# Layer 0's softmax weights made once: exponentials from the masked scores that VectorE keeps, turned by TensorE, in place of a second pass of scores

## The chip, the cores and the metric

The kernel runs on one core of a Trainium2 chip. A core has a matrix engine (TensorE, PE in the profile, with its weight loads as PEld), a vector engine (VectorE, DVE), an activation engine (ScalarE, ACT), a general engine (GpSimd, POOL) and a queue that issues transfers (SyncE, SP). Matrix products are written into PSUM, which has eight banks of 128 x 512 numbers; everything else works on SBUF. All data are 32-bit floats.

The metric is the device time of one execution in microseconds (us), the median of several runs.

## The reference, cut to what matters

Sixteen samples of 100 tokens (E = 512) pass through four layers, with a context of 361 rows for each sample. Layer 0, the only one that is changed, is a cross attention with 32 query heads in 8 groups that share keys and values, heads of 16:

```python
q = hidden_state @ Wq + bq                      # (16, 100, 512) -> 32 heads of 16
k = encoder_hidden_state @ Wk + bk              # (16, 361, 128) -> 8 heads of 16
v = encoder_hidden_state @ Wv + bv
scores = einsum('bkgld,bksd->bkgls', q, k) * scale + mask
attn = softmax(scores, axis=-1)                 # over the 361 context rows
out = einsum('bkgls,bksd->bkgld', attn, v) @ Wo + bo
x = layer_norm(out + hidden_state) * gamma + beta
```

Layers 1 and 3 are recurrent layers with a feed-forward part, layer 2 is a second cross attention with its own feed-forward. They read x as the layer ahead left it.

## The kernel before, in words

`layer0` (L238) loops over the 16 samples `b`. The queries of four samples (a group) are projected together; keys and values are projected for each sample. The 32 heads are ordered by a parity `par` (2), a chunk `q` (4) and a row group `r` (4): four heads `r` lie in four bands of 32 partitions of one tile, so that their four products run at once on four bands of PE. Four such products are called a burst here.

Before, the scores are made twice. The first pass (`maxima`, L376, eight calls for each sample, one for each `par` and `q`) makes a burst of scores 100 tokens x 361 rows; DVE adds the mask, negates, and keeps only the minimum of each row in the tile `nm`, while the masked scores go to a tile `junk` that nobody reads. `turn_maxima` (L397) turns these numbers by PE. The second pass (`weights`, L406, six calls: two parities, three blocks `j` of 121 rows) makes the scores again the other way round, with the context rows on partitions, subtracts the maximum by a second product (`msel`, `nx`) in the same bank, DVE adds the turned mask (`turn_mask`, L361), and one exponential of 121 x 1600 on ACT makes the weights `pt` of four `r` and four `q`. `attend` (L446) multiplies them with the values. The sums of the weights are made by POOL, which adds the three blocks into `pa`, and by PE (`sums`, L462, with the selector `osel`); DVE inverts them and `divide` (L484) spreads them over the channels by a product with `rsel`. `output` (L501) projects, adds the residual and normalizes.

The two passes are one sample apart: while sample `b` has its second pass, sample `b + 1` has its first. The list `ORDER` (L576) sets that order: S0 to S7 are first-pass calls, T0 to T5 second-pass calls. Ahead of the loop, the eight first-pass calls of sample 0 run alone.

All layer-0 work is recorded in program order on its engine (`mm`, `turn` and the wrappers `vector`, `scalar`, `gpsimd`, which is why nearly all rows in the profile carry the lines L77, L82 and L85). What is neither first nor second pass (projections, attends, sums, divide, output) is put into a `Filler` (L91): a list of pieces with an estimated time and the first slot in which each may stand. After each pass call the filler emits as many pieces as an equal share of the estimated total allows, and the deferred readers of their results in later slots.

PSUM in layer 0: a ring of six banks for scores (L242), one for the attended values `acc`, one for everything else. A burst takes the next four banks of the ring and writes them in the order r = 3, 2, 1, 0 (`BURST`); DVE reads them in the order 0, 1, 2, 3.

Transfers are issued by SP in program order: at the start of sample `b` the context, mask and x of sample `b + 2`.

Of the kernel before, what the change touches and what calls it, by code (L numbers as in the profile page):

```python
# [35 lines left out]
def xattn_sequence(ctx: ExitStack, tc: tile.TileContext, d: dict, out: bass.AP):  # L36
# [201 lines left out]
    def layer0(next_weights):  # L238
        with ExitStack() as es:
            one = es.enter_context(tc.tile_pool(name="l0_one", bufs=1))  # L240
            two = es.enter_context(tc.tile_pool(name="l0_two", bufs=2))
            score = psum_ring(es, "l0_sc", 6)  # L242
# [13 lines left out]
            i32 = ident.rearrange("p (r s) -> p s r", s=32)  # L256

            msel = one.tile([128, 2, KW], F32, name="l0_msel")


            osel = one.tile([KW, 8, 32], F32, name="l0_osel")

            rsel = one.tile([128, 4, 128], F32, name="l0_rsel")
            vzs = [one.tile([KW, 3, 2, 128], F32, name=f"vz{i}") for i in range(2)]
            nms = [one.tile([L, 4, 128], F32, name=f"nm{i}") for i in range(2)]

            live, qzs, xTs, last = {}, {}, {}, {}
# [53 lines left out]
            def keys(fill, b, slot=0):  # L321
                def ps():
                    live[b]["kz"] = two.tile([128, 2, S2], F32, tag="kz", bufs=3, name=f"kz_{b}")
                    t = bank(f"k_{b}")
                    return t, t[:, :S2]

                def then(t):
                    for par in range(2):
                        scalar.activation(
                            live[b]["kz"][:, par, :], t[:, :S2], AF.Identity,  # L330
                            bias=kb[:, par : par + 1], scale=par01[:, par : par + 1],
                        )

                chain(
                    fill, 0.63, slot, ps, lambda c: wk[:, c, :], lambda c: live[b]["ct"][:, c, :], then,
                    delay=0,
                )
# [23 lines left out]
            def turn_mask(fill, b, slot=0):  # L361
                mt = []

                def step():
                    mt.append(bank(f"mT_{b}"))
                    for j, (k0, _) in enumerate(KEYS):
                        turn(mt[0][:KW, j * L : (j + 1) * L], live[b]["mask"][:, k0 : k0 + KW], ident[:L, :L])

                def then():
                    t = live[b]  # L370
                    t["maskT"] = two.tile([KW, 3, L], F32, tag="maskT", bufs=3, name=f"maskT_{b}")
                    scalar.copy(t["maskT"].rearrange("p j t -> p (j t)"), mt[0][:KW, : 3 * L])

                fill.add(0.5, slot, step, then, 0, object())

            def maxima(b, x):  # L376

                par, q = x // 4, x % 4
                mask, kz = live[b]["mask"], live[b]["kz"]
                nm, qz = nms[b % 2], qzs[b // G]  # L380
                sl = slice(b % G * L, (b % G + 1) * L)
                ss = [score() for r in range(4)]
                for r in BURST:
                    rs = slice(32 * r, 32 * r + 32)
                    mm(
                        out=ss[r][:L, :S2], lhsT=qz[rs, q, sl], rhs=kz[rs, par, :],
                        start=True, stop=True,
                    )
                for r in range(4):
                    junk = two.tile([L, S2], F32, tag="junk", bufs=1, name=f"junk_{b}_{par}_{q}_{r}")  # L390
                    col = 32 * r + par
                    vector.tensor_tensor_reduce(
                        out=junk, in0=ss[r][:L, :S2], in1=mask, scale=-1.0, scalar=FLT_MAX,
                        op0=ALU.add, op1=ALU.min, accum_out=nm[:, q, col : col + 1],
                    )

            def turn_maxima(b):  # L397

                ps = bank(f"nmT_{b}")
                for q in BURST:  # L400
                    turn(ps[:, q * L : (q + 1) * L], nms[b % 2][:, q, :], ident[:L, :L])
                live[b]["nx"] = two.tile([128, T], F32, tag="nx", bufs=1, name=f"nx0_{b}")
                scalar.copy(live[b]["nx"], ps[:, :T])
                live[b]["pt"], live[b]["pa"] = {}, {}

            def weights(fill, b, k):  # L406


                par, j = k // 3, k % 3
                t = live[b]  # L410
                k0 = KEYS[j][0]
                sl = slice(b % G * L, (b % G + 1) * L)
                pt = t["pt"][k] = two.tile([KW, 4, T], F32, tag="pt", bufs=7, name=f"pt0_{b}_{k}")
                st = [score() for r in range(4)]
                for r in BURST:
                    rs = slice(32 * r, 32 * r + 32)
                    mm(
                        out=st[r][:KW, :T], lhsT=t["kz"][rs, par, k0 : k0 + KW],
                        rhs=qzs[b // G][rs, :, sl], start=True, stop=False,
                    )  # L420
                for r in range(4):
                    rs = slice(32 * r, 32 * r + 32)
                    mm(
                        out=st[r][:KW, :T], lhsT=msel[rs, par, :], rhs=t["nx"][rs, :],
                        start=False, stop=True,
                    )
                for r in range(4):
                    vector.tensor_tensor(
                        pt[:, r, :].rearrange("p (q t) -> p q t", t=L),
                        st[r][:KW, :T].rearrange("p (q t) -> p q t", t=L),  # L430
                        t["maskT"][:, j, None, :].to_broadcast([KW, 4, L]), ALU.add,
                    )

                def exp():
                    scalar.activation(pt, pt, AF.Exp)
                    if j == 1:
                        pa = t["pa"][par] = two.tile([KW, 4, T], F32, tag="pa", name=f"pa_{b}_{par}")
                        gpsimd.tensor_tensor(pa, t["pt"][k - 1], pt, ALU.add)
                    elif j == 2:
                        n = KEYS[2][1]  # L440
                        pa = t["pa"][par]
                        gpsimd.tensor_tensor(pa[:n], pa[:n], pt[:n], ALU.add)

                fill.later.append((fill.slot + 1, exp))

            def attend(fill, b, k, slot):  # L446
                par, j = k // 3, k % 3
                n = KEYS[j][1]

                def step():  # L450
                    if k == 0:
                        live[b]["acc"] = ps_acc.tile([128, 512], F32, tag="acc", name=f"acc_{b}")
                    for r in range(4):
                        rs = slice(32 * r, 32 * r + 32)
                        mm(
                            out=live[b]["acc"][rs, :T], lhsT=vzs[b % 2][:n, j, par, rs],
                            rhs=live[b]["pt"][k][:n, r, :], start=(k == 0), stop=(k == 5),
                        )

                fill.add(0.8, slot, step)  # L460

            def sums(fill, b, par, slot):  # L462
                def step(q):
                    for r in range(4):
                        rs = slice(32 * r, 32 * r + 32)
                        mm(
                            out=live[b]["acc"][rs, T : T + L], lhsT=osel[:, 4 * par + q, :],
                            rhs=live[b]["pa"][par][:, r, q * L : (q + 1) * L],
                            start=(par == 0 and q == 0), stop=(par == 1 and q == 3),
                        )  # L470

                def then():
                    t = live[b]
                    t["rinv"] = two.tile([128, L], F32, tag="rinv", name=f"rinv_{b}")
                    vector.reciprocal(t["rinv"], t["acc"][:, T : T + L])
# [3 lines left out]
                for q in range(4):  # L479
                    fill.add(  # L480
                        0.25, slot, lambda q=q: step(q), then if par == 1 and q == 3 else None, 0
                    )

            def divide(fill, b, slot):  # L484
                rb = []

                def step():
                    rb.append(bank(f"rb_{b}"))
                    for q in range(4):
                        mm(  # L490
                            out=rb[0][:, q * L : (q + 1) * L], lhsT=rsel[:, q, :], rhs=live[b]["rinv"],
                            start=True, stop=True,
# [6 lines left out]
                fill.add(1.0, slot, step, then, 1, object())  # L499

            def output(fill, b, slot):  # L501
# [6 lines left out]
                def then(t):  # L508
                    v = two.tile([L, E], F32, tag="v", bufs=1, name=f"res0_{b}")
                    vector.tensor_tensor(v, t[:L, :], xb[b], ALU.add)  # L510
                    st["v"], (st["mv"], st["rstd"]) = v, ln_stats(two, [v], 1e-6, f"0_{b}", vector, gpsimd)
                    fill.later.append((fill.slot + 5, scaled))
# [29 lines left out]
            m2 = one.tile([128, 2], F32, name="l0_m2")  # L542
            vector.tensor_reduce(m2, i32[:, 0:2, :], AX.X, ALU.add)
            vector.tensor_copy(msel, m2[:, :, None].to_broadcast([128, 2, KW]))
            for t in nms + vzs + [osel]:
                gpsimd.memset(t, 0.0)
            for i in range(8):
                gpsimd.memset(osel[:, i, i : i + 1], 1.0)
                vector.tensor_copy(
                    rsel[:, i % 4, :].rearrange("p (r h c) -> p h r c", h=2, c=16)[:, i // 4],  # L550
                    i32[:, i, :, None].to_broadcast([128, 4, 16]),
                )
            gpsimd.memset(osel[:, 0, 8:32], 1.0)
# [6 lines left out]
            turn_mask(fill, 0)  # L560
# [1226 lines left out]
```

## Time and profile before

| What | us |
|---|---|
| Median of three runs | 3452.1 (3450.18 to 3452.9) |
| Profiled execution | 3447.39 |
| Its span in the profile | 3445.6 |
| First scores of layer 0 | 29.1 |
| First pass over sample 1 begins (loop starts) | 66.0 |
| Turned maxima of sample 0, of sample 15 | 66.8, 690.8 |
| Last row of layer 0 ends, layer 1 begins | 739.1 |

Busy times over the whole span: PE 3121.5 us (91%), DVE 1753.5 (51%), ACT 977.3 (28%), POOL 1373.2 (40%).

In the rows of the timeline, the first number is the start in us from the begin of the span, the second the time from the first start to the last end, then engine, line, operation, output<-inputs, the shapes and how many instructions were merged; in brackets the idle time of the engine ahead of it and what ended it. A product of 32-bit floats is two matmul instructions, a transposition is one. In the windows, each engine's busy time in a stretch is followed by its number of instructions; PEclk is the clock granted to PE, as a share of full speed. Matmul ends are modelled and overlap, so the cost of a group on PE is best read from its start to the next group's start.

### The profile page before, as it was taken

How to read it: one execution, taken by the hardware profiler on the slowest of the kernel's cores; microseconds unless marked ns; L12 is line 12 of the kernel's file. 1: busy time of each engine (PE TensorE's matmuls, PEld its weight loads, DVE VectorE, ACT ScalarE, POOL GpSimd, SP SyncE). 2: the span in 40 equal slices, each digit the busy share in tenths (PEclk: the TensorE clock that was granted, in tenths of full speed). 3: DMA queues.
4: the chain of work that ended last, by engine and by line, in shares of the span. 5: the costliest groups of instructions: out<-in, count | busy, mean ns of one | idle time of the engine just before them, and what ended most of it. 6: DMA issues, size and time to landing. Idle time of an engine off the chain costs nothing. (4 is left out here: it accounts for less than half of the span.)

```text
span 3445.6 us, 47937 instructions
## 1 busy us (share of the span) xinstructions
PE 3121.5 (91%) x18371; PEld 1422.0 (41%) x18371; DVE 1753.5 (51%) x3570; ACT 977.3 (28%) x1715; POOL 1373.2 (40%) x1036
## 2 busy tenths in 40 slices
PE   6989898868999989988999999879998899998997
PEld 3434443334333333334455555445553433333333
DVE  4777777732877766523333333320001287766661
ACT  1333233222233333321323222211111233423332
POOL 0444444443775765521212111220002377676551
PEclk8999999979999989999999999989998999998998
DMA  5010100013335353222000000010011343535321
GB/s 173 22 31 22 31 22 34 1 32 115 113 108 150 109 173 108 77 72 64 28 19 20 19 20 31 26 64 10 10 58 34 111 129 102 150 116 174 91 70 50
DMA packets 171374, 240.18 MB, mean 70 GB/s; under 512 B 27678, under 2 KB 139358, under 8 KB 171146
## 3 DMA queue, kind: packets, MB, share of 16 engines
q1 hardware_dynamic: 148106, 204.35, 19.9%
q10 hardware_dynamic: 23040, 32.78, 2.7%
q8 instruction: 144, 2.36, 0.3%
q14 instruction: 84, 0.69, 0.1%
HBM read 174.25 MB, written 36.04 MB: 61 GB/s over the span
## 5 line engine op out<-in xcount | busy, mean ns | idle before, releaser
L77 POOL TENSOR_TENSOR a<-a,rr 128x800 f32<-128x800 f32 x256 | 480.9, 1880 | 331.0 <-DVE a L77 212.0
L77 DVE TENSOR_TENSOR_SCAN a<-wr,vb 128x400 f32<-128x400 f32 x512 | 475.9, 971 | 20.7 <-PE acc L82 9.1
L77 DVE TENSOR_TENSOR vb<-vb,kr 128x792 f32<-128x792 f32 x256 | 250.1, 977 | 184.7 <-ACT vb L77 184.5
L77 DVE CUSTOM_DVE_ANT_0 junk<-l_sc,mask 100x361 f32<-100x361 f32 x512 | 272.9, 533 | 87.1 <-PE l_sc L82 70.5
L82 PE MATMUL vb<-vc,sel 32*128 32x396 f32 x1024 | 252.7, 565 | 3.3 <-DVE a L77 3.3
L77 DVE TENSOR_TENSOR pt<-l_sc,maskT 121x400 f32<-121x400 f32 x384 | 193.4, 566 | 89.6 <-PE l_sc L82 88.8
L77 ACT ACTIVATE pt<-pt 121x1600 f32<-121x1600 f32 x96 | 147.6, 1538 | 282.4 <-DVE pt L77 280.8
L1490 DVE CUSTOM_DVE_ANT_0 junk<-l2a_sc,mask 100x361 f32<-100x361 f32 x256 | 136.9, 535 | 173.0 <-PE l2a_sc L82 155.8
L1526 POOL TENSOR_TENSOR pa<-pt,pt 121x1600 f32<-121x1600 f32 x16 | 57.1, 3569 | 362.3 <-ACT pt L1521 362.3
L77 POOL TENSOR_TENSOR xj<-tm,ext 128x400 f32<-128x400 f32 x160 | 150.6, 961 | 110.9 <-DVE tm L77 110.1
L77 DVE SCALAR_TENSOR_TENSOR tm<-mm,vec,sx 128x400 f32<-128x400 f32 x160 | 95.7, 628 | 185.5 <-PE mm L82 149.4
L82 PE MATMUL k<-ct,l_k_w 128*128 128x361 f32 x512 | 173.3, 482 | 14.4 <-DMA ct<-in_ctxT 14.4
L1707 DVE TENSOR_TENSOR x<-pb,x 100x512 f32<-100x512 f32 x16 | 12.2, 760 | 335.4 <-DMA pb<-po 330.3
L77 POOL TENSOR_TENSOR pa<-pt,pt 121x1600 f32<-121x1600 f32 x32 | 114.7, 3583 | 165.0 <-ACT pt L77 165.0
L63 PE MATMUL h<-yTb,l_fc 128*128 128x400 f32 x512 | 174.5, 503 | 6.3 <-ACT yTb L229 6.3
L82 PE MATMUL v<-l_v_w,ct 128*121 128x512 f32 x384 | 175.5, 601 | 0.0
L63 PE MATMUL p<-l_proj,h 128*128 128x512 f32 x384 | 165.5, 592 | 0.0
L77 ACT COPY vb<-s0r 128x8 f32<-128x8 f32 x256 | 42.9, 168 | 407.8 <-PE vb L82 320.4
L82 PE MATMUL l_sc<-kz,qz 32*100 32x361 f32 x1024 | 116.7, 526 | 42.9 <-DVE pt L77 22.0
L82 PEld LDWEIGHTS vb<-vc,sel 32*128 32x128 f32 x1024 | 81.9, 191 | 154.0 <-issue 113.5
L63 PEld LDWEIGHTS h<-yTb,l_fc 128*128 128x128 f32 x512 | 97.7, 192 | 81.1 <-ACT yTb L229 8.3
L77 POOL TENSOR_TENSOR pa<-pa,pt 119x1600 f32<-119x1600 f32 x32 | 114.4, 3576 | 41.1 <-ACT pt L77 40.9
(258 smaller groups left out, 5174.2 us busy)
## 6 DMA issues: line engine op xcount, KB each, us to landing
kr<-dk SPq DMA_DIRECT2D x256, 100.0 KB
wr<-dw SPq DMA_DIRECT2D x256, 100.0 KB
rr<-dr SPq DMA_DIRECT2D x256, 100.0 KB
ct<-in_ctxT SPq DMA_DIRECT2D x32, 722.0 KB
dk<-k ACTq DMA_DIRECT2D x32, 200.0 KB
kc<-dk SPq DMA_DIRECT2D x32, 200.0 KB
dw<-wd ACTq DMA_DIRECT2D x32, 200.0 KB
dv<-v ACTq DMA_DIRECT2D x32, 200.0 KB
```

The lines of the kernel that those rows point to most:

```text
L63: nc.tensor.matmul(out=ps, lhsT=lhs(c), rhs=rhs(c), start=(c == 0), stop=(c == n - 1))
L77: return lambda *args, **kw: tc.keep_in_program_order(op(*args, **kw))
L82: pin(nc.tensor.matmul(**kw))
L1490: nc.vector.tensor_tensor_reduce(out=junk, in0=ss[r][:L, :S2], in1=t["mask"], scale=-1.0, scalar=FLT_MAX, op0=ALU.add, op1=ALU.min, accum_ ...
L1526: nc.gpsimd.tensor_tensor(t["pa"], t["pt"][0], pt, ALU.add)
L1707: nc.vector.tensor_tensor(x, pb[:, i, :], x, ALU.add)
```

## The change: what it does

The second pass of scores goes, and with it `turn_mask`, `turn_maxima`, `sums`, the selectors `msel`, `osel` and `rsel` and POOL's additions. DVE's pass writes the negated masked scores into a tile `pr` (three buffers) instead of `junk`; its minima go to `nm`, 32 columns for a sample. ACT then makes the weights in place, one exponential of 100 x 361 for each head, with scale -1 and the minimum as bias, and its accumulator gives the sum of each row into `sums`. PE turns the weights (`turn_weights`): for each of the eight calls and each of the three blocks `j`, four transpositions of 100 x 121 into one bank of a new ring of two (`l0_pT`). ACT copies blocks 0 and 2 into `pt`, DVE copies block 1. `attend` is as before. `invert` inverts the 32 sums of a token on DVE, POOL spreads them over 16 channels each (`rx`), and `divide` turns that by PE.

The score ring has four banks instead of six; the two others are the new ring. The loop goes over the samples once, one burst for each of eight steps x, with the turning of a step one step behind; a seventeenth pass through the loop finishes the last sample. There is no run of sample 0 ahead of the loop: values of samples 0 and 1, keys of sample 1 and the product of the value bias stand in the first sample. Keys have two buffers instead of three and are made one sample ahead instead of two.

```diff
-            score = psum_ring(es, "l0_sc", 6)
+            score = psum_ring(es, "l0_sc", 4)
+            turned = psum_ring(es, "l0_pT", 2)
...
+            def scores(b, x):
                 par, q = x // 4, x % 4
...
                 ss = [score() for r in range(4)]
                 for r in BURST:
                     rs = slice(32 * r, 32 * r + 32)
                     mm(
+                        out=ss[r][:L, :S2], lhsT=qzs[b // G][rs, q, sl], rhs=t["kz"][rs, par, :],
                         start=True, stop=True,
                     )
+                pr = two.tile([L, 4, S2], F32, tag="pr", bufs=3, name=f"pr_{b}_{x}")
+
+                def maximum(r):
+
+                    col = 8 * q + 2 * r + par
+                    vector.tensor_tensor_reduce(
+                        out=pr[:, r, :], in0=ss[r][:L, :S2], in1=t["mask"], scale=-1.0, scalar=FLT_MAX,
+                        op0=ALU.add, op1=ALU.min, accum_out=t["nm"][:, col : col + 1],
+                    )
+
+                def exp(r):
+                    col = 8 * q + 2 * r + par
+                    scalar.activation(
+                        pr[:, r, :], pr[:, r, :], AF.Exp, bias=t["nm"][:, col : col + 1], scale=-1.0,
+                        accum_out=t["sums"][:, col : col + 1],
+                    )
+
+                return pr, maximum, exp
+
+            def turn_weights(b, x, pr, j):
+
+                par, q = x // 4, x % 4
+                t = live[b]
+                if q == 0 and j == 0:
+                    t["pt", par] = two.tile([KW, 3, 4, T], F32, tag="pt", name=f"pt0_{b}_{par}")
+                ps = turned()
+                k0 = KEYS[j][0]
                 for r in range(4):
+                    turn(ps[:KW, r * L : (r + 1) * L], pr[:, r, k0 : k0 + KW], ident[:L, :L])
+                return lambda copy: copy(
+                    t["pt", par][:, j, :, q * L : (q + 1) * L],
+                    ps[:KW, :T].rearrange("p (r t) -> p r t", t=L),
+                )
...
+            def invert(b):
+
+                t = live[b]
+                rinv = two.tile([L, 32], F32, tag="rinv", name=f"rinv_{b}")
+                vector.reciprocal(rinv, t["sums"])
+                t["rx"] = two.tile([L, E], F32, tag="rx", bufs=1, name=f"rx_{b}")
+                gpsimd.tensor_copy(
+                    t["rx"].rearrange("p (h c) -> p h c", c=16), rinv[:, :, None].to_broadcast([L, 32, 16])
+                )
...
+                for x in range(8):
+                    now = (b, x, *scores(b, x)) if b < B else None
+                    if now:
+                        pr, maximum, exp = now[2:]
+                        maximum(0)
+                        maximum(1)
+                    due = fill.run(3 * x, due + share)
+                    if last:
+                        turn_weights(*last[:3], 0)(scalar.copy)
+                    if now:
+                        exp(0)
+                        exp(1)
+                        maximum(2)
+                    due = fill.run(3 * x + 1, due + share)
+                    if last:
+                        turn_weights(*last[:3], 1)(vector.tensor_copy)
+                    if now:
+                        maximum(3)
+                    if last:
+                        turn_weights(*last[:3], 2)(scalar.copy)
+                    if now:
+                        exp(2)
+                        exp(3)
+                    last = now
+                    due = fill.run(3 * x + 2, due + share)
+                    if x == 0 and prev:
+                        invert(b - 1)
```

## The prediction

> **What bounds the kernel now.** The page's chain of work cannot be used here: it breaks off at 2238 us, far behind layer 0, which alone is changed. I read the timeline first, for the borders: the first scores start at 29.1 us, the first pass over the sample loop at 66, and layer 1 starts on the last row at 739.1. Then the windows between these borders:
>
> ```profile
> core 0: us, PE busy (x) PEld busy (x) DVE busy (x) ACT busy (x) POOL busy (x), PEclk, DMA share, GB/s
> 29.10:65.95 36.85, 25.18 (x135) 13.55 (x134) 17.32 (x64) 3.69 (x9) 0.00 (x0) 0.77 0.54 192
> 66.80:690.80 624.00, 551.18 (x4874) 247.40 (x4870) 480.92 (x1403) 185.55 (x201) 274.30 (x129) 0.98 0.07 23
> 690.80:739.10 48.30, 33.76 (x316) 15.75 (x316) 18.76 (x37) 10.59 (x9) 27.62 (x16) 0.85 0.06 23
> ```
>
> The middle row is 15 samples of 41.6 us. PE is busy 88% of it, 36.75 us a sample; DVE 77%, ACT 30%, POOL 44%, DMA 7%. PE bounds, with 4.85 us of waiting a sample. The first row is a run-in that only makes the maxima of sample 0 and projections; there DVE and then one product after the other set the time. The last row is sample 15 and the serial end.
>
> The timeline within a sample shows what a burst costs and what frees the next one:
>
> ```profile
> 305.93 0.87 PE L82 MATMUL l_sc<-kz,qz 32*100 32x361 f32 x8 [0.41 <-DVE pt L77]
> 306.73 0.88 PE L82 MATMUL acc<-pt,vz 121*32 121x400 f32 x8
> 308.84 0.54 DVE L77 CUSTOM_DVE_ANT_0 junk<-l_sc,mask 100x361 f32<-100x361 f32 x1
> 309.30 0.08 DVE L77 DVE_READ_ACCUMULATOR2_ANT nm<- 100x1 f32 x1
> 309.44 0.95 PE L82 MATMUL l_sc<-qz,kz 32*121 32x400 f32 x8 [0.29 <-DVE nm L77]
> ```
>
> A burst of four scores holds PE 0.80 us (start to next start), an attend 0.81. A maximum with its accumulator read comes every 0.58 us. The burst at 309.44 starts when the second of four maxima has been read: with six score banks, a burst needs only two to come free, and its round trip lies under the other two maxima. What a transposition costs:
>
> ```profile
> 57.73 0.39 PEld L85 LDWEIGHTS mT<-ident,mask 100*121 100x121 f32 x3 [1.86 <-ACT kz L77]
> 57.73 0.56 PE L85 MATMUL mT<-ident,mask 100*121 100x100 f32 x3 [1.29 <-ACT kz L77]
> 58.32 0.41 ACT L77 COPY maskT<-mT 121x300 f32<-121x300 f32 x1 [0.65 <-PE mT L85]
> ```
>
> The tile's row gives 269 ns for one in the stream. So the third of three starts 0.29 us after the first: about 0.18 to the second, 0.105 to each one after; the copy starts 0.30 after the last one's start, and another matmul could start about 0.20 after it.
>
> **The change, part by part.** I count a sample, then a step (a sample has eight: one parity, one q, four r).
>
> *PE.* Removed a sample, start to next start in the timeline: the second scores and the products that subtract the maximum, 6 x (0.77 + 0.78) = 9.3 us; 64 instructions of sums, 32 in 0.82, so 1.65; the turned maxima 0.55 (four in 0.53); the turned mask 0.49; the product that spreads 1/sum, 1.07. Together 13.06. Added a step: a first group of four transpositions, 0.18 + 2 x 0.105 + 0.20 = 0.60, and a second and third that stand together in the built order, 0.18 + 6 x 0.105 + 0.20 = 1.01; eight steps are 12.9 us, and turning 1/sum adds 0.55. So PE work goes from 36.75 to 36.75 - 13.06 + 13.45 = 37.1 us a sample, 4.64 a step: nothing is won there.
>
> *DVE.* The 24 additions a sample (0.50 us each busy) go, eight copies of 121x400 come. The trace has no such copy on DVE; the addition of that shape (0.57 alone, 0.50 in a stream) is nearest, ACT's 0.49 the other end; I take 0.50. The 100x128 reciprocal (0.77) becomes one of 100x32, bounded by 0.16 (a DVE reduce to two elements) and 0.77, once a sample beside PE. A step of DVE is 4 x 0.58 + 0.50 + 0.35 (residual, statistics, scaling, y: 2.8 us a sample) = 3.2 us.
>
> *ACT.* The six exponentials of 1.54 go; 32 of 100x361 come. Layer 2's exponential of 121x400 with a bias column takes 0.594 alone and 0.51 in a stream, so 0.48 at 361. The accumulated sum has no row on ACT: DVE's read shows 0.04 net, ACT's smallest copy (128x8) 0.168. I take 0.10, 0.58 together. A step: 4 x 0.58 + two copies of 0.49 + 0.34 (kz, vz, y, qz: 2.7 us a sample) = 3.6 us, 3.4 to 3.9 by the bounds. It stays under PE's 4.64.
>
> *POOL.* 64 additions of 3.57 us vanish; they cost a 3.0 us wait of PE once, at 723.4. The spreading of 1/sum (100x512; the nearest row, the residual add, 1.27 us) and a small clear come; from the first step to the divide in the second or later there is over one step of cover, and at the end the last three attends (2.4 us) cover it. DMAs are the same in number and place; the context is released earlier (its values are made in the same sample), and DMA is 7% busy: nothing.
>
> *The new waits.* The score ring falls to four banks, and the burst writes r = 3 first, whose bank is read last. So a burst cannot start before the last maximum of the step before: the round trip, 31.14 (last read) to 31.19 to 0.93 us later on DVE (29.09 to 30.02), is now bare, 0.98 us a step: DVE's loop is 3.2 + 0.98 = 4.2 us, still under 4.64. Between the third and the fourth maximum DVE waits for the second group of transpositions: from that group's end 0.20 + 0.50 + 0.58 + 0.05 = 1.33 us pass until the next burst may start. PE has in that time the third group (0.52) and whatever filler stands behind it. In the built order of sample 5 a piece (0.7 to 1.05 us) stands there in seven of eight steps; in samples 3, 7, 14, without queries, in four to five. A step without one waits 0.8 us: 0.8 x 2.5 / 8 = 0.25 on average. I add 0.2 for steps whose first group follows the burst at once and meets the last exponential (ends about 0.7 us after the last maximum, the burst at 0.8), and for the third group's bank (ACT's copy). That makes 4.64 + 0.46 = 5.1 us a step, 40.8 a sample. Before, PE waited 0.61 a step.
>
> *The run-in.* Its 32 maxima now lie in the ordinary first sample, with k, both v, queries and the value bias: 6.4 (bursts) + 12.9 + 3.2 + 5.6 + 2.4 + 5.8 + 3.6 = 40 us of PE, taken as 43 with waits. The last sample has no projections ahead of it: DVE's loop sets it, 36 us. The end, by the rows from 718 to 739 without POOL's addition: 1.2 exponentials, 1.6 groups, 0.5 copy, 2.4 attends, 0.5 y, 0.6 and 0.6 divide, 4.5 output, 6 to the last row: 18.
>
> Sum: 29.1 + 43 + 14 x 40.8 + 36 + 18 = 697 us, for 739: 42 less, of which the run-in gives about 30 and the loop 12. Layer 1 starts on the last row (the timeline names POOL x), and what follows is untouched, so all of it counts. The profiled execution took 3447.4 around a span of 3445.6; the median of the runs is 4.7 above it. 3452.1 - 41 = **3411 us**.
>
> **Rivals.**
>
> *PE never waits* (4.64 a step): 29 + 41 + 14 x 37.1 + 33 + 18 = 640, 98 less, 3354. For it: in seven of eight steps filler covers the chain; against: before, with two banks spare, PE waited 4.85 us a sample. Chance 0.12.
>
> *ACT sets the step.* If the accumulator read is a full ACT instruction after a drained exponential, 0.594 - 0.03 + 0.17 = 0.73, ACT has 4.25 us, plus the trip through PE between a step's last exponential and the copy that opens the next on ACT (0.105 + 0.30 + 0.05 to about 1.2 when PE first has filler to finish): about 5.3 a step, 42.4 a sample, 22 us worse than my sum: 3433, still faster. For it: ACT's order puts that copy ahead of all four exponentials. Chance 0.15.
>
> *Slower: the transposition's copy holds the ring.* Its place is the copy on DVE between the third and fourth maximum. If the filler of a step (2.3 us) falls ahead of the second group, the step is a serial chain: 0.80 + 0.60 + 0.42 + 2.3 + 1.33 = 5.45, and 5.8 when DVE's other work (0.35) falls into it too. At 5.8: 29 + 46 + 14 x 46.4 + 38 + 18 = 781, 42 more, 3494. It decides from 5.45 a step on, where the sum reaches 739. For it: samples 3 and 7 with three or four bare steps; against: sample 5. Chance 0.15.
>
> *Slower: the clock.* In the run-in, one burst per four maxima with idle PE between, the granted clock was 0.50 from 36 to 49 us, where PE was busy 68% at that clock, so 34% at full; from 66 to 110 it was busy 72% at 0.96. If the waits of each step brought the 0.81 of 700 to 800 us, a step would be 4.64 / 0.81 + 0.46 = 6.2, and the layer 29 + 50 + 14 x 49.6 + 40 + 20 = 833, 94 longer: 3546. After the change PE should be busy 90%, so the rows speak against it. The Trainium skill (TensorE: Matmul & The Clock Gate, "A second HAM failure mode: psum-queue depth-cycling") states that short idle times between groups, from cycling PSUM banks, can make the clock swing between half and full; the rows of 100 to 600 us, with such waits at a clock of 0.97 to 1.00, don't show it. Chance 0.06.
>
> **How the numbers follow.** My case has 0.52, PE without waits 0.12, ACT 0.15, the held ring 0.15, the clock 0.06. About 0.2% (7 us) is what a measurement of this kernel tells from no change: of ACT's case 0.02 and of the ring's 0.03 fall within it. Faster 0.52 + 0.12 + 0.13 = 0.77, same 0.05, slower 0.12 + 0.06 = 0.18. My own case spans 4.9 to 5.3 a step (14 x 8 x 0.2 = 22 us each way), 3389 to 3433. The range of 8 in 10 takes in ACT's case, part of PE's and the milder half of the ring's: 3370 to 3465.
>
> **What would show it.** Layer 1's first row near 697; steps of 5.1 us from burst to burst; PE 90% busy; transpositions 0.105 apart; each burst released by the last maximum's read; the copy on DVE waiting for PE; exponentials with their reads 0.52 to 0.65 apart. Wrong would be: bursts waiting over 1 us in most steps, ACT busy above 80%, or a clock under 0.9 between 100 and 600 us.

## The result and the profile after

The changed kernel takes 3373.2 us (median of four runs, 3358.7 to 3374.0) where the kernel before takes 3451.1 (3448.5 to 3452.9): a ratio of 0.9765, 95% interval 0.9746 to 0.9785, so 78 us or 2.35% faster. Forecast were 41 us, a time of 3411; the range 3370 to 3465 holds the result, near its lower end. The profiled execution took 3373.7 us with a span of 3371.9.

Layer 1's first row starts at 662.4 us, for 739.1 before and about 697 forecast: layer 0 is 76.7 us shorter. All that follows took 2709.4 us, 2706.5 before, so the gain lies in layer 0 alone.

The windows of the changed kernel, between the same kind of borders as before (first sample, 14 samples, last sample with the end); the columns are those of the prediction's first table:

```profile
core 0: us, PE busy (x) PEld busy (x) DVE busy (x) ACT busy (x) POOL busy (x), PEclk, DMA share, GB/s
28.50:71.30 42.80, 37.46 (x257) 23.14 (x256) 19.12 (x71) 28.78 (x87) 0.00 (x0) 1.00 0.49 165
71.30:602.80 531.50, 491.70 (x3609) 290.78 (x3608) 312.67 (x1092) 394.32 (x1197) 73.10 (x98) 1.00 0.08 26
602.80:665.00 62.20, 47.85 (x268) 25.22 (x268) 28.65 (x113) 28.86 (x88) 10.78 (x16) 0.76 0.06 22
```

| Piece | forecast | measured |
|---|---|---|
| first scores to the second sample's first burst | 43 | 42.8 |
| 14 samples | 571.2 (40.8 each, 5.1 a step) | 531.6 (37.97 each, 4.746 a step) |
| last sample and the end, to layer 1's first row | 54 | 59.6 |

The middle row is nearly the whole difference: 39.6 us less than forecast. PE is busy 92.5% of it, 35.1 us a sample (37.1 forecast), and idles 0.36 us a step (0.46 forecast). DVE is at 59%, ACT at 74%, and the clock is full.

The timeline shows the chain that the prediction named, here in a step with nothing behind the third group:

```profile
279.79 1.01 PE L85 MATMUL l_pT<-ident,pr 100*121 100x100 f32 x8
280.49 0.57 DVE L77 COPY pt<-l_pT 121x400 f32<-121x400 f32 x1 [1.29 <-PE l_pT L85]
280.98 0.52 DVE L77 CUSTOM_DVE_ANT_0 pr<-l_sc,mask 100x361 f32<-100x361 f32 x1
281.43 0.08 DVE L77 DVE_READ_ACCUMULATOR2_ANT nm<- 100x1 f32 x1
281.56 0.87 PE L82 MATMUL l_sc<-kz,qz 32*100 32x361 f32 x8 [0.76 <-DVE nm L77]
```

The eight transpositions are the second and third group together. DVE's copy starts 0.70 after the first of them, the fourth maximum 0.49 later, its read 0.45 later, and the burst 0.13 after that: 1.77 us from the first transposition to the burst. PE had nothing else to do for 0.76 us.

The instructions by group, DVE and then ACT (busy time, mean of one in ns, idle time before it and what ended that), 71 to 602 us:

```profile
L77 DVE CUSTOM_DVE_ANT_0 pr<-l_sc,mask 100x361 f32<-100x361 f32 x447 | 220.0, 528 | 109.1 <-PE l_sc L82 108.9
L77 DVE COPY pt<-l_pT 121x400 f32<-121x400 f32 x112 | 64.3, 574 | 109.2 <-PE l_pT L85 50.2 <-ACT pr L77 48.2 <-ACT pt L77 10.7
...
L77 ACT ACTIVATE pr<-pr,nm 100x361 f32<-100x361 f32 x446 | 262.4, 593 | 0.2 <-POOL sums L77 0.2
L77 ACT COPY pt<-l_pT 121x400 f32<-121x400 f32 x223 | 109.1, 489 | 128.2 <-PE l_pT L85 127.3
L77 ACT ACTIVATION_READ_ACCUMULATOR pr<-pr,nm 100x1 f32 x446 | 85.8, 192 | 0.0
```

The exponential and its read overlap their neighbours: from one exponential's start to the next are 0.59 us (0.58 forecast).

### The profile page after: what moved, and what is told of

Read it like the earlier page. It is cut to its first block, busy times and chain, and to the rows that moved or that the text cites. A ratio compares the mean times of both kernels' runs of the same rounds, so it can differ in the third digit from the quotient of the medians.

```text
span 3371.9 us, 46386 instructions
## 1 busy us (share of the span) xinstructions
PE 3091.1 (92%) x17171; PEld 1484.4 (44%) x17171; DVE 1593.4 (47%) x3304; ACT 1229.8 (36%) x2867; POOL 1154.0 (34%) x992
## 5 line engine op out<-in xcount | busy, mean ns | idle before, releaser
L77 DVE CUSTOM_DVE_ANT_0 pr<-l_sc,mask 100x361 f32<-100x361 f32 x512 | 252.0, 528 | 147.6 <-PE l_sc L82 147.4
L77 ACT ACTIVATE pr<-pr,nm 100x361 f32<-100x361 f32 x512 | 301.2, 593 | 1.1 <-DVE nm L77 0.9
L85 PEld LDWEIGHTS l_pT<-ident,pr 100*121 100x121 f32 x1536 | 195.7, 188 | 103.9 <-issue 51.9
L85 PE MATMUL l_pT<-ident,pr 100*121 100x100 f32 x1536 | 218.3, 278 | 5.2 <-ACT pt L77 4.1
L1478 POOL TENSOR_TENSOR pa<-pt,pt 121x1600 f32<-121x1600 f32 x16 | 57.1, 3572 | 362.3 <-ACT pt L1473 362.3
L77 ACT COPY pt<-l_pT 121x400 f32<-121x400 f32 x256 | 125.3, 489 | 151.4 <-PE l_pT L85 150.5
```

What stands on the lines that cost most here:

```text
L77: return lambda *args, **kw: tc.keep_in_program_order(op(*args, **kw))
L85: pin(nc.tensor.transpose(out, in_, ident))
L1478: nc.gpsimd.tensor_tensor(t["pa"], t["pt"][0], pt, ALU.add)
```

## The experiments

Two theories stood against each other on what is left of PE's waiting. A: the chain second group, DVE's copy, fourth maximum, next burst. B: ACT, which is 74% busy and in the rows above ends part of DVE's waits. Where a few us matter, I give the time from the second sample's first burst to the last sample's first burst, divided by its 112 steps. This step of the loop is the same, to 0.001 us, in two profiled executions of the changed kernel:

> The changed kernel once more, on the same chip as the small added operation, for the difference between the two: 3365 to 3376, a step of 4.74 to 4.76 us.

Measured: 3358.4 us, ratio to before 0.9757 (0.9722 to 0.9792), a step of 4.747. The step is as expected, the time is not: it lies about 7 us under the expected 3365, and also under the 3370 at which the prediction's range begins. Outside the loop the two executions differ: the last sample and the end took 51.1 us here and 59.6 in the first one, the rest of the program 2698.6 and 2709.4. So single differences of 10 us in the whole time mean little, and the step is the better witness.

**One operation more, at two places of DVE's order.**

```diff
+            late = one.tile([L, S2], F32, name="l0_late")
...
                     if last:
                         turn_weights(*last[:3], 1)(vector.tensor_copy)
                     if now:
+                        vector.tensor_copy(late, live[b]["mask"])
                         maximum(3)
```

> The changed kernel with one more DVE operation in every step (a copy of the mask, 100x361, into a tile that nobody reads), placed between the copy of the second group of transpositions and the fourth maximum. The kernel computes what it did. The added operation is taken as 0.4 us (between the 0.46 of a maximum and 0.3). Theory A (the chain: second group of transpositions, DVE's copy, fourth maximum, next burst): what is put into this chain shows. PE waits 0.35 us a step now, so about half of the steps have no slack; 0.2 to 0.4 us a step x 112 steps = 22 to 45 us longer than the changed kernel, 3395 to 3418. Theory B (PE's remaining waits come from ACT's exponentials and copies, DVE is covered): 0 to 6 us longer, since DVE goes from 59% to 67% busy only.

For the other place, the same line stands behind `maximum(1)`:

> The same added DVE operation (the mask copied into a tile that nobody reads) in every step, but placed behind the second maximum, ahead of the third. The kernel computes what it did. Theory A: DVE stands there with time in hand, since it has to wait for the second group of transpositions anyway; 0 to 10 us longer than the changed kernel, 3373 to 3383. Theory C (it is DVE's load as such, not the place in the chain): as much as with the operation in the other place, 22 to 45 us. Theory B: 0 to 6 us, or more if ACT's third exponential, which becomes later by 0.4 us, sets the step.

Measured: late 3401.9 us, ratio 0.9870 (0.9849 to 0.9891), a step of 5.087; early 3371.5, ratio 0.9783 (0.9768 to 0.9797), a step of 4.759. The kernel with the late operation, in its timeline:

```profile
282.85 0.99 PE L85 MATMUL l_pT<-ident,pr 100*121 100x100 f32 x8
283.53 0.57 DVE L77 COPY pt<-l_pT 121x400 f32<-121x400 f32 x1 [1.85 <-ACT pr L77]
283.68 0.80 PE L82 MATMUL k<-ct,l_wk 128*128 128x361 f32 x2
284.02 0.34 DVE L77 COPY l_late<-mask 100x361 f32<-100x361 f32 x1
284.27 0.53 DVE L77 CUSTOM_DVE_ANT_0 pr<-l_sc,mask 100x361 f32<-100x361 f32 x1
284.86 0.27 PEld L82 LDWEIGHTS l_sc<-kz,qz 32*100 32x100 f32 x8 [0.96 <-DVE nm L77]
```

Late, the operation costs 0.34 us a step; early, 0.01, although DVE then does the same amount (its busy share in the window of the 14 samples goes from 59% to 64%). It is the place that counts, not the load.

The 0.34 is not the operation's length alone. Step by step against the changed kernel, the 112 steps are 38.2 us longer. In 92 of them the fourth maximum starts 0.25 us later and the step grows by 0.17 on average: by the whole 0.25 in 50 steps, by less or nothing in nearly all others. 9 steps, with 15.2 of the 38.2 us, meet something else: the granted clock, 1.00 in the whole loop of the changed kernel, falls to half eight times for 3.4 us. In the other 11, the added copy meets a longer operation of POOL and lasts up to 0.95 us instead of 0.34; the next experiment shows how. The window of the 14 samples, which had a clock of 1.00 in the changed kernel, reads here:

```profile
71.30:602.80 531.50, 475.80 (x3361) 277.38 (x3359) 319.28 (x1114) 367.84 (x1113) 66.69 (x90) 0.97 0.08 26
```

**A small operation at the late place** asks whether there is slack that swallows a little. The edit is the same with `late[:, :32]` and the first 32 columns of the mask.

> The changed kernel with a small DVE copy (100x32 of the mask, read by nobody) in every step, between the copy of the second group of transpositions and the fourth maximum; by the copy of 128x32 in layer 1 it takes about 0.17 us, in a stream perhaps 0.12. The prediction took a maximum to be 0.12 longer than it is at this place. Theory A, without slack: as with the larger operation at the same place, the step grows by the operation's whole length, 0.10 to 0.17 us x 112 = 11 to 19 us longer in the profile's loop. A threshold instead (slack that swallows a small operation): 0 to 5 us.

Measured: 3385.4 us, ratio 0.9824 (0.9795 to 0.9852), beside the changed kernel's 3358.4 on the same chip; a step of 4.886, so 0.140 more. On average the fourth maximum starts 0.639 us after the copy, for 0.491 without the operation: 0.148 later, which looks like an exact match. Step by step it is not. In 95 of the 112 steps the maximum is 0.08 later, and the step grows by 0.08 in 49 of them, by nothing in 38, and by 0.04 on average: about half of the steps have slack, and in the others what the chain gets longer, the step gets longer. Of the 15.7 us in all, only 3.6 come from these 95 steps. 8.5 come from 15 steps in which the added copy starts while POOL works on 100x512 numbers, and ends only when POOL has ended:

```profile
192.05 1.26 POOL L77 TENSOR_TENSOR x<-res,l_rows 100x512 f32<-100x512 f32 x1
192.09 1.26 DVE L77 COPY l_late<-mask 100x32 f32<-100x32 f32 x1
193.27 0.52 DVE L77 CUSTOM_DVE_ANT_0 pr<-l_sc,mask 100x361 f32<-100x361 f32 x1
```

There the chain is 0.57 us longer on average, and the step too. The last 3.5 us come from two steps with the clock at half.

**The fourth maximum ahead of the copy.**

```diff
-                    if last:
-                        turn_weights(*last[:3], 1)(vector.tensor_copy)
+                    copy1 = turn_weights(*last[:3], 1) if last else None
                     if now:
                         maximum(3)
+                    if last:
+                        copy1(vector.tensor_copy)
```

> The changed kernel with the fourth maximum ahead of DVE's copy of the second group of transpositions; nothing is added or removed. Theory A: the burst is freed 0.57 us (the copy) earlier, and no longer hangs on the transpositions. PE waits 0.35 us a step in all; if most of it is this chain, 0.15 to 0.3 us a step x 112 = 17 to 34 us shorter than the changed kernel, 3339 to 3356. Theory B: no change, 3370 to 3376, or a few us longer, because the bank of the second group comes free later.

Measured: 3333.0 us, ratio 0.9674 (0.9658 to 0.9690), below the changed kernel's interval. The step falls to 4.495, by 0.251; PE idles 0.134 in it instead of 0.356. The step that was shown above for the changed kernel now looks so:

```profile
273.44 0.53 DVE L77 CUSTOM_DVE_ANT_0 pr<-l_sc,mask 100x361 f32<-100x361 f32 x1
273.90 0.08 DVE L77 DVE_READ_ACCUMULATOR2_ANT nm<- 100x1 f32 x1
274.12 1.01 PE L85 MATMUL l_pT<-ident,pr 100*121 100x100 f32 x8
274.81 0.57 DVE L77 COPY pt<-l_pT 121x400 f32<-121x400 f32 x1 [0.84 <-PE l_pT L85]
275.06 0.87 PE L82 MATMUL l_sc<-kz,qz 32*100 32x361 f32 x8
```

The whole maximum lies ahead of the copy. The burst starts 0.94 us after the first transposition, for 1.77, and PE did not wait for it. So 0.22 of the 0.36 us of waiting in a step was this chain.

**No sums on ACT** (a kernel that leaves out the softmax's sums).

```diff
-                    gpsimd.memset(t["sums"], 0.0)
+                    gpsimd.memset(t["sums"], 1.0)
...
                         pr[:, r, :], pr[:, r, :], AF.Exp, bias=t["nm"][:, col : col + 1], scale=-1.0,
-                        accum_out=t["sums"][:, col : col + 1],
```

> The changed kernel without the accumulator on ACT's exponentials; the sums of the softmax in layer 0 are left out (all are set to 1), so that the attention is not normalised there. The 512 accumulator reads of ACT vanish. Theory A: ACT (74% busy) is covered; 0 to 6 us shorter than the changed kernel, 3367 to 3373. Theory B: 32 x 0.09 = 2.9 us a sample less on the engine that PE waits for, as much as PE's whole waiting (2.8 us a sample); 20 to 39 us shorter, 3334 to 3353.

Measured: 3352.9 us, ratio 0.9733 (0.9709 to 0.9757). By the ratios that is 11 us under the changed kernel, and the median lies at the edge of what B expected; but the step is 4.693, 0.053 less, which is 6 us in the loop, as A expected at most. Another 9 us of layer 0 lie in the last sample and the end, 50.7 us, where the second execution of the unedited kernel also took only 51.1. So ACT's reads are covered for the most part: of the 0.36 us a step that they take from ACT, 0.05 show.

**Filler early: nothing behind the third group.**

```diff
-                    due = fill.run(3 * x, due + share)
+                    due = fill.run(3 * x, due + 1.5 * share)
...
-                    due = fill.run(3 * x + 1, due + share)
+                    due = fill.run(3 * x + 1, due + 1.5 * share)
...
-                    due = fill.run(3 * x + 2, due + share)
+                    due = fill.run(3 * x + 2, due) if b == B else due
```

> The changed kernel with all its filler pieces (projections, attends, divide) in the first two places of a step and none behind the third group of transpositions; the same instructions in another order. Theory A: behind the second group PE has only the third group (0.4 to 0.6 us) as cover for the copy, the fourth maximum and their ends (0.20 + 0.57 + 0.46 + 0.05 = 1.28), so that every step waits about 0.7 instead of 0.35; 0.3 to 0.7 us a step x 112 = 34 to 78 us longer than the changed kernel, 3407 to 3451. A rival in which PE's work alone sets the step: no change, 3370 to 3380.

Measured: 3427.9 us, ratio 0.9932 (0.9913 to 0.9951); a step of 5.301, 0.555 more. PE's waits for the maximum, from the view of waits between 75 and 570 us (total, times, longest), first in the changed kernel and then with early filler:

```profile
PE l_sc L82 <- DVE nm L77: 21.6, 28, 1.1
```

```profile
PE l_sc L82 <- DVE nm L77: 69.7, 92, 1.1
```

Nearly every burst now waits, and most by 0.76 us. Here too the clock falls to half for 3.4 us in the loop, seven times; by the longer times of the products in these stretches I estimate this at 0.09 of the 0.555.

**Both edits together.**

> The two edits together: the fourth maximum ahead of DVE's copy, and all filler in the first two places of a step. Theory A: once the burst no longer hangs on the transpositions, the place of the filler ceases to matter for it; within 0 to 12 us of the kernel with the fourth maximum first alone (3333), that is 3333 to 3345. If the loss by early filler has another cause (ACT's copies, the banks of the transpositions), it comes in full here too: 34 to 78 us above 3333.

Measured: 3325.2 us, ratio 0.9643 (0.9618 to 0.9669); a step of 4.453. The very edit that costs 0.555 us a step in the changed kernel gains 0.04 here. The waits for the maximum are gone, the clock is full again, and PE is busy 98% of the loop. So the loss by early filler hung on the chain; a loss by ACT's copies or by the banks of the transpositions would have come here too. This kernel computes all that the reference does and is the shortest of all that ran: 126 us below before, and by the ratios 42 below the changed one.

**PE's price.** In the kernel with the maximum first, the first group of each step is made twice:

```diff
-                for r in range(4):
+                for r in (0, 1, 2, 3) * (2 if j == 0 else 1):
                     turn(ps[:KW, r * L : (r + 1) * L], pr[:, r, k0 : k0 + KW], ident[:L, :L])
```

> The kernel with the fourth maximum ahead of DVE's copy, and the first group of each step's transpositions made twice (the same four into the same bank, eight instead of four). It prices the work of PE. PE is busy 97% there. If four more transpositions cost 4 x 0.105 = 0.42 us a step and all of it shows: 128 x 0.42 = 54 us above 3333, 3387. If each four carry the 0.60 that the prediction used, 77 us, 3410. If PE's work is covered by another engine: 0 to 15 us.

Measured: 3382.7 us, ratio 0.9800 (0.9778 to 0.9823); a step of 4.863, 0.368 more than with the maximum first alone, while PE's idle time falls from 0.134 to 0.109. So four transpositions more are 0.368 + 0.025 = 0.393 us of PE work, 0.098 each (0.105 forecast), and with PE 98% busy nearly all of it shows. The four stand inside a group; what a group costs at its borders this kernel does not tell.

**The kernel before, with two buffers for the scores that nobody reads.** DVE's maxima come 0.455 us apart in the changed kernel, in a stream, and 0.576 apart before, though one takes about the same (528 and 533 ns). In the built program, each maximum before waits for DVE's own semaphore of the one ahead, which writes the same tile `junk`; those that write `pr` do not.

```diff
-                    junk = two.tile([L, S2], F32, tag="junk", bufs=1, name=f"junk_{b}_{par}_{q}_{r}")
+                    junk = two.tile([L, S2], mybir.dt.bfloat16, tag="junk", bufs=2, name=f"junk_{b}_{par}_{q}_{r}")
```

> The kernel before, whose maxima write their unused masked scores into two buffers in turn instead of one (of half as wide a type, so that both fit in the same room). Only the unused output changes. Theory D: in the kernel before each maximum waits for the end of the one before it because both write the one buffer, and that is why its maxima come 0.58 us apart and those of the changed kernel 0.46; with two buffers they come 0.45 to 0.47 apart here too, DVE has 32 x 0.12 = 3.8 us a sample less, bursts are freed earlier by 0.12 to 0.24, and the kernel is 10 to 30 us shorter than before. Rival: the spacing belongs to the operation in that kernel (source, bank or neighbours); 0.57 to 0.58 as before and no change of the time beyond 5 us.

Measured: 3434.1 us, ratio 0.9948 (0.9929 to 0.9967), so 17 us faster than before. The timeline of before, then of this kernel:

```profile
300.43 0.54 DVE L77 CUSTOM_DVE_ANT_0 junk<-l_sc,mask 100x361 f32<-100x361 f32 x1
300.89 0.08 DVE L77 DVE_READ_ACCUMULATOR2_ANT nm<- 100x1 f32 x1
301.01 0.54 DVE L77 CUSTOM_DVE_ANT_0 junk<-l_sc,mask 100x361 f32<-100x361 f32 x1
```

```profile
307.22 0.51 DVE L77 CUSTOM_DVE_ANT_0 junk<-l_sc,mask 100x361 bf16<-100x361 f32 x1
307.64 0.08 DVE L77 DVE_READ_ACCUMULATOR2_ANT nm<- 100x1 f32 x1
307.64 0.53 DVE L77 CUSTOM_DVE_ANT_0 junk<-l_sc,mask 100x361 bf16<-100x361 f32 x1
```

With one buffer the next maximum starts 0.12 us after the read of the last; with two it starts with it, and the median distance is 0.455. The edit also halves the width of the output. The operation takes 533 ns in both, and the changed kernel has the short distance at full width, so the width is not needed for it. A kernel with two buffers at full width was not run. Not all of the 17 us need be this wait: between 66 and 690 us the granted clock was 0.99 here, for 0.98 in the loop before.

The Trainium skill (VectorE: DVE Perf Modes, "The DRAIN you can't avoid") states that a semaphore after each DVE copy costs nothing extra, because the next operation waits for the pipeline to empty anyway. These rows are of another operation, a maximum with an accumulator read, and they differ: without the wait the next maximum begins 0.08 us before the end of the one ahead, with it 0.04 us after, and for this operation the measurement decides.

## Why the prediction was right in its mechanism and wrong in its size

*What was right.* The sign, and the mechanism: PE bounds the loop, the burst waits for the last maximum, and that one hangs on the second group of transpositions through DVE's copy. ACT's exponential with its sum (0.59 for 0.58), the copy (0.49 to the next start for 0.50) and the wait of a step without filler behind the third group (0.76 for 0.8) were sized well. That the first sample took 42.8 for 43 is luck in part: PE's work there was 37.5 for 40, and its waits 5.3 for 3.

*The step that failed* is the loop's, "4.64 + 0.46 = 5.1 us a step": it measures 4.39 + 0.36 = 4.75. Both terms were too large, PE's work above all.

- PE's work was put 0.25 us a step too high, 28 us in 112 steps. The transpositions are 11.9 us a sample for 12.9, and turning 1/sum takes 0.37 for 0.55. I gave each group an opening of 0.18 and a closing of 0.20, from a single row (`mT`). From group start to the next start in the timeline, a group of four between two projections takes 0.405 us and one of eight 0.83, without either. A product in bands of 32 next to the group (an attend or a burst) adds 0.09 to 0.10 on its side: four behind a projection and ahead of an attend take 0.50, and eight between two attends 1.02. Only with such products on both sides is a group as long as I had every group:

```profile
288.50 0.57 PE L85 MATMUL l_pT<-ident,pr 100*121 100x100 f32 x4
289.00 0.88 PE L82 MATMUL acc<-pt,vz 121*32 121x400 f32 x8
289.80 1.09 PE L85 MATMUL l_pT<-ident,pr 100*121 100x100 f32 x8
290.82 0.88 PE L82 MATMUL acc<-pt,vz 121*32 121x400 f32 x8
...
297.37 0.57 PE L85 MATMUL l_pT<-ident,pr 100*121 100x100 f32 x4
297.78 0.86 PE L82 MATMUL q<-xT,l_wq 128*128 128x400 f32 x2
298.48 0.99 PE L85 MATMUL l_pT<-ident,pr 100*121 100x100 f32 x8
299.30 0.86 PE L82 MATMUL q<-xT,l_wq 128*128 128x400 f32 x2
```

- The rest of PE's excess, 0.9 a sample, lies in the work that stays, 22.8 for 23.7. 0.2 of this is that the removed products had been 13.3 in the window before, not 13.06. Most of the other 0.6 is the clock. The prediction read a mean of 0.98 in the loop before as a full clock, but it is seven stretches of 3.4 us at half clock, and a key matmul takes 0.63 us to the next start in them, for 0.37 elsewhere. By such times I estimate 9 us in the 15 samples before. They were in the 36.75 from which the prediction started, and the loop of the changed kernel has none. One of the stretches before:

```profile
341.90:345.30 3.40, 3.40 (x5) 1.16 (x4) 1.65 (x8) 0.73 (x1) 0.00 (x0) 0.50 0.00 0
```

- The waits were put 0.10 a step too high, 12 us. The bursts' wait for the maximum is 0.21 (21.6 us in 104 steps, in the view of waits above) for 0.25: about two steps in eight stand bare, for 2.5. The other waits are 0.15 for 0.2. The chain itself was nearly right, because two errors in it cancel: I took the maximum at 0.58, its distance in the kernel before, which held 0.12 us of a wait for the one buffer `junk`, and the way from there to the burst at 0.05; measured are 0.45 to its read and 0.13 from there.

28 and 12 us make up the 39.6 that the loop was shorter than forecast. (The forecast also took 41 us off where its own sum gives 42, which has no weight.) The last sample and the end were 5.6 us longer than forecast. The clock was at half there for 17 us from 607.3 us on, and an attend took 1.56 us instead of 0.88; in the second execution it was at half for 5.5, and the same stretch took 51.1.

*The rivals.* PE without waits (3354) did not come: 0.36 us a step remained. But one exchange of two lines makes it almost true, at 3333 and 3325, lower than that rival's sum because the PE work in it was the 4.64. ACT as the bound fell: its sums gave back only 0.05 of the 0.36 us a step that the read was thought to cost. The copy that holds the ring is a true mechanism, and early filler calls it up: the rival's serial chain was 5.45; measured are 5.30. The changed kernel does not reach it because filler falls behind the third group in most steps. At that chain it would still have been faster than before (0.9932), not slower. The clock stayed at 1.00 in the 14 samples, with PE waiting 0.36 us in a step and cycling through banks, so this rival fell. But the prediction's reading that the rows before show no swing was wrong: four of the seven stretches at half clock lie between 100 and 600 us, under means of 0.97 and 0.98. The Trainium skill (TensorE: Matmul & The Clock Gate, "A second HAM failure mode: psum-queue depth-cycling") tells of a kernel whose clock swings between half and full with short idle times of this kind. In the runs here such stretches are found in the loops where PE waits most: none at up to 0.36 us of waiting a step, two with the small late operation (0.45), three in the kernel before with two buffers (0.52), eight with the late operation (0.56), seven in the kernel before (0.61) and with early filler (0.85). That the waits cause them is likely but not shown.

*What the gain consists of.* The prediction put 30 us of its 42 to the run-in. Measured by step: 14 samples cost 41.6 each before and 37.97 after, 51 us of the 76.7; the run-in, the first and the last sample give the other 26. Of the 51, 28 are waits (4.85 a sample before, 2.84 after) and 23 are PE's work (36.75 and 35.12), about 8 of these by the clock.

## What to carry to other kernels

When the next product waits for the last of several reads of its banks, put nothing between these reads that waits for another engine: here one copy moved behind the last maximum was worth 0.25 us a step, 28 us in the loop, and it made the place of the filler unimportant. Before a duration is taken over into a chain, look whether it is the operation or the distance to its neighbour, and what makes the distance: a scratch tile with one buffer, read by nobody, put 0.12 us between maxima. Price a group of small products by what stands on both sides of it, not by one row that stands alone. Before a busy time is taken over, look at the clock in its window: a mean of 0.98 held 9 us. And when an added operation is to show the price of a wait, compare step by step: a mean can agree for other reasons.

## What was not expected of the hardware

- A write to the same tile by successive DVE operations put 0.12 us between them (0.576 against 0.455); the kernel before with two buffers, of half the width, was 17 us shorter.
- Four transpositions of 100x121 between products on the whole array take 0.405 us; a product in bands of 32 ahead of them or behind them adds 0.09 to 0.10 each (0.50 with one, 0.595 with both).
- A DVE copy from SBUF to SBUF that started while POOL worked on 100x512 numbers ended only behind it: 17 of the 128 small copies took 0.39 to 1.26 us instead of 0.17, and each ended 0.03 to 0.11 us after a POOL operation of 1.26 us that was under way when it began.
- ACT's read of its accumulator is an instruction of 192 ns, of which 0.09 us shows: exponentials come 0.590 apart in a stream with it and 0.498 without (the kernel without sums).
- The step of the loop repeats to 0.001 us between executions (4.746, 4.747), while the last sample and the end differ by 8.5 us and the rest of the program by 10.8.
